# A four-layer convolution network on one core: results held until loads have come, foldings spread later, another order of the set-up, last masks on VectorE

## The chip, the cores and the metric

The kernel runs on one core of a Trainium2 chip. A core has a matrix engine (TensorE, "PE" in the profile; "PEld" is its loading of weights), a vector engine (VectorE, "DVE"), a scalar engine (ScalarE, "ACT"), a general engine (GpSimd, "POOL") and an engine that here only issues transfers (SyncE, "SP"). Each runs its own list of instructions in order and waits at an instruction until what it needs is there. Transfers between DRAM and the core's memory are issued by SP, ACT or POOL and are carried out by 16 DMA engines that they share. PE writes its products to PSUM, a small memory of eight banks; ACT and DVE take them out.

The metric is device time in microseconds (us). Eight runs of the kernel before took 3073.03 to 3084.0 us, with a median of 3080.26 us.

## The reference

The input x has 1024 images of 16 x 16 pixels and 16 channels (float32). Four layers follow one another, each added to its input; ahead of each stands a normalisation by groups of two channels per image.

```python
x = x + L0(gn(x))   # tensor-train matrix on the 16*16*16 values: three cores of rank 16
x = x + L1(gn(x))   # depthwise filters, dense 48->128, relu, dense 128->16, mask
x = x + L2(gn(x))   # 3x3 convolution, 16 -> 16 channels, and a bias
x = x + L3(gn(x))   # as L1, with other weights

def _gn(v, G=8, eps=1e-5):          # mean and variance over height, width and 2 channels
    return (g - m) / jnp.sqrt(s + eps)

def update(x):                      # layers 1 and 3, one step
    p = concat([xt, depthwise(xt, conv1), depthwise(xt, conv2)])   # 48 channels
    d = relu(p @ fc0_w.T + fc0_b) @ fc1_w.T + fc1_b
    xn = xt + d
    return xn * (alive(xt) & alive(d))   # alive: 3x3 maximum of channel 3 above 0.1
```

## The kernel before, in words

**Data.** The images are cut into two chunks of 512. A chunk is 32 "lines" of 128 partitions by 512 images (256 KB each). Two big buffers of 32 lines, X0 and X1 (`XN`), hold a chunk each; between layers the results lie in DRAM (`xf[1]` to `xf[4]`; `xf[3]` is the same memory as `xf[2]`, layer 2 adds to it in place).

**How the order comes about.** The order on every engine is the order in which the program writes the instructions. `run` (from line 1478) takes a layer as a list of steps of PE, and lays background lists (loads, norms, preparation of weights) between them: each background step has a cost or is a pause, and is written out when the layer's steps have come to its share of the window given. Pauses are shrunk so that they fill at most 0.7 of the window. `now` writes a list out at once. All that is fixed is the order on each engine: an engine that is not held up by data runs ahead of the others.

**Set-up** (lines 1529 to 1546). SP loads x of chunk 0 in eight pieces of 1 MB; DVE takes statistics of each (`stat`, L833). `setup[0]` transposes the weights of layer 0; `setup[1:]` are the sums of `c0` on POOL (L535 to L541) and eight steps `gs` that multiply two cores (PE L560, ACT L564) and store the result (SP L569). `lines[0]` and `lines[1]` turn the pixels of the upper and lower half into lines: four transposes on PE (L839) and a copy on ACT (L842, which stays in X0, or L850), and POOL stores them to `xr` (L844, L852). `tail` makes the norm's factors: `small` (DVE aggregate L864, ACT root L866), `newton`, two `widen` (DVE L880), two `spread` (PE L888, ACT L889). Then `start` builds the first weights (PE L1020, ACT L1025, DVE L1038), and `normed` (DVE L910) makes the input of the first product (PE L1097). PSUM's tag `w` has four banks, which the copies of transposes, of `pg`, of `pw` and of the foldings share in turn.

**Layer 0** runs in five phases of 16 units. In phase 1 (160 steps of two products) the weights of layers 1 and 3 are prepared in the background: `beside(make1, make3)` alternates the steps of both layers. The first eight of each are inputs, two dense ones, bias lines and rows, `taps` (DVE L331, POOL L335 and L337), `order` (POOL L350, L359) and `xpats` (POOL L321 to L324). Then eleven foldings follow, each a `make` (PE L392 into two banks, ACT L398 into a buffer `e`) and a `send` (2 to 16 transfers by POOL, L404, 80 per layer). Each layer has three buffers `e`, used in turn, so a folding's copy waits until the sends of the folding three before it have landed. The buffers lie in X1; at 0.75 of the phase SP loads the next part into X1 (L939).

**Layers 1 and 3** (`layer_nca`) work through 32 tiles a chunk, (q, w2) with q from 0 to 3 and w2 from 0 to 7: products L1465, relu on ACT L1468, products L1318, DVE adds bias and input (`u`, L1330), and `residual` multiplies by the mask and adds to the tile fetched from DRAM, both on POOL (L1367, L1368). Some steps later SP stores the tile (L1370); in the last chunk of layer 3 PE transposes it instead (L1377), DVE copies it (L159), and SP stores the output (L1607).

**Layer 2** (`layer_conv`) has 16 rows h a chunk. PE multiplies (L1192 and, across the halves, L1201), ACT adds the bias and writes a result `r` (L1240; twelve buffers), and POOL sends it with an accumulating transfer to `xf[2]` (L1243). The program writes the sends out late, from h = 5 on, but nothing else stands between them on POOL. Beside chunk 0 SP loads chunk 1 into X1 (16 pieces of 512 KB, L784) and DVE and ACT normalise it: sum of all pieces (L598, L606, L614), mean on PE (L693), subtraction (L639), squares, variance (L697). Beside chunk 1 the next layer's chunk 0 is loaded into X0 (L791) and normalised by quarters (L722, L726, L738).

Of the kernel before, what the change touches and what calls it, by code (L numbers as in the profile page):

```python
# [12 lines left out]
ALU = mybir.AluOpType  # L13
# [9 lines left out]
NL = 32  # L23
# [80 lines left out]
def conv_preact_kernel(ctx: ExitStack, tc: tile.TileContext, a: dict, out: bass.AP):  # L104
    nc = tc.nc
    V, A, G, T = nc.vector, nc.scalar, nc.gpsimd, nc.tensor
# [9 lines left out]
    xf = [  # L116
        [dram.tile([8, 4, P, NB], F32, tag=f"xf{l}_{n}", name=f"xf{l}_{n}") for n in range(NCH)]
        for l in range(5)
    ]
# [45 lines left out]
    def cst(name, shape, dt=F32):  # L165
        return const.tile(shape, dt, tag=name, name=name)
# [249 lines left out]


    b2 = cst("b2", [P, 1])

    convw = cst("convw", [P, 512])  # L420

# [360 lines left out]
    def load_wc(X, src):  # L782
        return [
            lambda wh=wh, h=h: nc.sync.dma_start(X[:, 16 * wh + h : 16 * wh + h + 2], rows_wc(src, wh, h, 2))  # L784
            for wh in range(2)
            for h in range(0, S, 2)
        ]

    def load_cw(X, src):
        return [  # L790
            lambda q=q, w=w: nc.sync.dma_start(  # L791
                X[:, 8 * q + w : 8 * q + w + 2], src[w : w + 2, q].rearrange("w p b -> p w b")
            )
            for q in range(4)
            for w in range(0, 8, 2)
        ]
# [5 lines left out]
    def rows_wc(t, wh, h, n=1):  # L802

        t = t[4 * wh : 4 * wh + 4].rearrange("w q (c h) b -> (w q c) h b", h=S)
        return t[:, h : h + n]
# [347 lines left out]
        hw=convw[:, 384:512].rearrange("p (n e m) -> p n e m", n=2, e=2),  # L1153
    )

    def layer_conv(X, n):

        st = {}  # L1160
# [70 lines left out]

            return go

        waiting = []

        def finish(h):

            for wh in range(2):
                r = work([P, NB], "r", "conv")
                A.activation(r, st["po", h][wh], AF.Identity, bias=b2)  # L1240
                waiting.append((rows_wc(xf[2][n], wh, h), r.unsqueeze(1)))
            while waiting and 2 * h + 2 - len(waiting) < 4 * (h - 4):
                G.dma_start(*waiting.pop(0), accum_op=ALU.add)  # L1243

        steps = []
        for h in range(0, S, 2):
# [10 lines left out]
    def layer_nca(X, n, l, L, xo=None):  # L1257


        st = {}  # L1260
# [103 lines left out]

        def residual(q, w2):
            u, r = st["u", q, w2], st["r", q, w2]
            G.tensor_tensor(u, u, st["m"][:, w2], ALU.mult)  # L1367
            G.tensor_tensor(r, r, u, ALU.add)  # L1368
            if xo is None:
                after(7, lambda: nc.sync.dma_start(tile_cw(xf[l + 1][n], 8 * q + w2), r))  # L1370
            else:
                after(8, lambda: turn(q, w2, r))
# [136 lines left out]
    def put(L):  # L1509
        return lambda: nc.sync.dma_start(pack, L["pack"])  # L1510
# [7 lines left out]
    def now(steps):  # L1518
        for step in steps:
            step = step[1] if isinstance(step, tuple) else step  # L1520
            if callable(step):
                step()

    def beside(xs, ys):

        pause = [12, 8, 1, 1, 6, 14, 10, 6] + [1] * (len(xs) - 8)
        return [z for x, y, t in zip(xs, ys, pause) for z in (x, 2.6, y, 2.6, t)]

    L1, make1 = nca_weights("L1_conv_", X1[:, 0:16])
    L3, make3 = nca_weights("L3_conv_", X1[:, 16:32])  # L1530
    with ExitStack() as es:
# [5 lines left out]

        A.activation(work([P, NB], "n", "warm")[:, 0:1], ident[:, 0:1], AF.Sqrt)
        now(setup[:1])
        now(stat[0] + stat[1])  # L1540
        now(setup[1:])
        now(lines[0][:4] + lines[1][:4] + tail[:3] + lines[0][4:10] + tail[3:])
        start, phases = layer_train()
        start()
        now(normed(0, 0, 1) + combined(0, True))
# [42 lines left out]
    with ExitStack() as es:  # L1588
        shared[0] = "m"
        stage(es, conv_sb, conv_ps)  # L1590
        run(layer_conv(X0, 0), 108, load_wc(X1, xf[2][1]), (norm_lines(X1), 0.09, 1.04), by=0.07)
        run(
            layer_conv(X1, 1), 108, load_cw(X0, xf[3][0]) + [put(L3)], (norm_cw(X0, True), 0.09, 1.06), by=0.07
        )
    with ExitStack() as es:
        shared[0] = "o"
# [41 lines left out]
```

## Time and profile before

| what | value |
|---|---|
| median of 8 runs | 3080.26 us (3073.03 to 3084.0) |
| profiled execution, its own time | 3077.39 us |
| its span, first to last instruction | 3075.7 us |
| mean granted clock of TensorE | 0.985 |
| PE busy | 2988.1 us (97%), 13746 instructions |
| PEld busy | 1250.5 us (41%) |
| DVE busy | 1756.8 us (57%) |
| ACT busy | 1099.8 us (36%) |
| POOL busy | 684.8 us (22%) |
| DMA | 418.67 MB, mean 136 GB/s |

How it is read: the stages lie at about 0 to 45 us (set-up), 45 to 1810 (layer 0; phase 1 from some 212 to 559), 1810 to 2296 (layer 1), 2296 to 2526 (layer 2), 2526 to the end (layer 3). A line of the timeline gives the start and length of a group of instructions in us, the engine, the line in the kernel, the operation, what it writes and reads, how many there are, and in brackets how long the engine stood before it and what ended that. A line of waits gives the waiting engine and line, what it waited for, the total, the number and the longest. "Issue" as a releaser means that the profile shows nothing that was waited for. DMA-issuing instructions of SP are not counted as busy.

### The profile page before, as it was taken

How to read it: one execution, taken by the hardware profiler on the slowest of the kernel's cores; microseconds unless marked ns; L12 is line 12 of the kernel's file. 1: busy time of each engine (PE TensorE's matmuls, PEld its weight loads, DVE VectorE, ACT ScalarE, POOL GpSimd, SP SyncE). 2: the span in 40 equal slices, each digit the busy share in tenths (PEclk: the TensorE clock that was granted, in tenths of full speed). 3: DMA queues.
4: the chain of work that ended last, by engine and by line, in shares of the span. 5: the costliest groups of instructions: out<-in, count | busy, mean ns of one | idle time of the engine just before them, and what ended most of it. 6: DMA issues, size and time to landing. Idle time of an engine off the chain costs nothing.

```text
span 3075.7 us, 36641 instructions
## 1 busy us (share of the span) xinstructions
PE 2988.1 (97%) x13746; PEld 1250.5 (41%) x13746; DVE 1756.8 (57%) x2330; ACT 1099.8 (36%) x1798; POOL 684.8 (22%) x738
## 2 busy tenths in 40 slices
PE   7999899999999999999999999999998999999996
PEld 5544334444444444444444433333333333333332
DVE  5264236555554555544555668656967766856432
ACT  4431331100000000000101156666676656666563
POOL 2125651200000000000000015434542223442332
PEclk8999999999999999999999999999999999999998
DMA  7644654533333433322222244435346756344555
GB/s 297 233 129 96 142 115 159 178 108 110 112 112 126 149 108 108 108 101 87 87 87 93 70 142 160 130 129 195 123 136 150 190 92 208 123 129 115 149 162 195
DMA packets 251809, 418.67 MB, mean 136 GB/s; under 512 B 35044, under 2 KB 105320, under 8 KB 248560
## 3 DMA queue, kind: packets, MB, share of 16 engines
q1 hardware_dynamic: 225376, 362.45, 35.8%
q0 software_dynamic: 25440, 53.58, 8.5%
q8 instruction: 109, 1.79, 0.2%
q14 instruction: 68, 0.56, 0.1%
q10 hardware_dynamic: 816, 0.30, 0.0%
HBM read 238.79 MB, written 165.60 MB: 131 GB/s over the span
## 4 chain that ended last, share of the span: by engine, by line
issue 47%; PE 34%; POOL 4%; DMA 1%; DVE 1%; SPq 0%; POOLq 0%; DVEq 0%
PE ph L1465 17%; PE po L1318 6%; PE po L1097 6%; PE po L1192 2%; POOL u L1367 2%; POOL res L1368 2%; POOL xf L1243 1%; PE ptx L1377 0%; PE L_conv_pe L392 0%; PE pw L1020 0%; PE pvar L726 0%; DMA xn<-xf 0%; PE pr L738 0%; PE pmean L722 0%; PE po L1201 0%
## 5 line engine op out<-in xcount | busy, mean ns | idle before, releaser
L1097 PE MATMUL po<-xn,w 128*128 128x512 f32 x3584 | 1579.2, 597 | 4.6 <-DVE xn L910 4.6
L1097 PEld LDWEIGHTS po<-xn,w 128*128 128x128 f32 x3584 | 671.0, 190 | 843.0 <-issue 820.3
L1468 ACT ACTIVATE hid<-ph,pack 128x512 f32<-128x512 f32 x1024 | 652.6, 686 | 381.3 <-PE ph L1465 271.7
L1133 DVE TENSOR_TENSOR r<-r,po 128x512 f32<-128x512 f32 x576 | 377.9, 683 | 593.2 <-PE po L1097 526.4
L1367 POOL TENSOR_TENSOR u<-u,mask 128x512 f32<-128x512 f32 x128 | 203.2, 1587 | 1817.1 <-DMA nx<-xn 1263.4
L1025 ACT COPY w<-pw 128x512 f32<-128x512 f32 (+1 forms) x320 | 150.6, 557 | 1189.3 <-issue 1003.4
L1465 PE MATMUL ph<-xn,wq 32*128 32x512 f32 x3664 | 567.8, 611 | 0.0
L1465 PEld LDWEIGHTS ph<-xn,wq 32*128 32x128 f32 x3664 | 233.2, 184 | 270.6 <-issue 237.6
L1465 PE MATMUL ph<-xn,pack 32*128 32x512 f32 x1288 | 298.8, 626 | 1.2 <-DVE mask L1363 0.9
L1318 PE MATMUL po<-hid,pack 128*32 128x512 f32 x2048 | 281.9, 605 | 2.7 <-ACT hid L1468 2.7
L1038 DVE TENSOR_TENSOR w<-w 128x512 f32<-128x512 f32 x320 | 210.3, 683 | 93.7 <-ACT w L1025 93.7
L639 DVE TENSOR_TENSOR xn<-xn,m 128x1024 f32<-128x1024 f32 x160 | 225.4, 1457 | 45.6 <-ACT m L654 45.5
L1368 POOL TENSOR_TENSOR res<-res,u 128x512 f32<-128x512 f32 x128 | 212.4, 1659 | 10.0
L1330 DVE SCALAR_TENSOR_TENSOR u<-po,pack,xn 128x512 f32<-128x512 f32 x128 | 95.9, 749 | 204.4 <-PE po L1318 200.3
L1192 PE MATMUL po<-xn,convw 128*128 128x512 f32 x368 | 166.6, 605 | 5.1 <-ACT conv L1240 5.1
L1465 PEld LDWEIGHTS ph<-xn,pack 32*128 32x128 f32 x1288 | 116.3, 186 | 98.9 <-issue 63.1
L1133 DVE TENSOR_TENSOR xn<-xn,po 128x512 f32<-128x512 f32 x96 | 64.3, 684 | 125.9 <-PE po L1097 125.8
L1318 PEld LDWEIGHTS po<-hid,pack 128*32 128x32 f32 x2048 | 42.8, 108 | 198.0 <-issue 138.2
L606 DVE TENSOR_TENSOR sq<-sq 128x1024 f32<-128x1024 f32 x78 | 106.9, 1370 | 13.9 <-ACT sq L624 11.7
L1192 PEld LDWEIGHTS po<-xn,convw 128*128 128x128 f32 x368 | 69.1, 193 | 102.7 <-issue 93.6
L1020 PE MATMUL pw<-R,gq 32*128 32x256 f32 (+1 forms) x1280 | 91.4, 385 | 13.2 <-ACT xn L398 10.9
L404 POOL DMA_DIRECT2D L_conv_wy<-xn x160 | 88.9, 563 | 42.4 <-ACT xn L398 31.7
(162 smaller groups left out, 1773.0 us busy)
## 6 DMA issues: line engine op xcount, KB each, us to landing
xf<-r SPq DMA_DIRECT2D x112, 512.0 KB, 3.9
xn<-xf SPq DMA_DIRECT2D x96, 512.0 KB, 5.2
r<-xf SPq DMA_DIRECT2D x80, 512.0 KB, 4.5
wq<-L_conv_wy SPq DMA_DIRECT2D x192, 192.0 KB, 2.8
res<-xf SPq DMA_DIRECT2D x128, 256.0 KB, 3.1
xf<-res SPq DMA_DIRECT2D x96, 256.0 KB, 2.0
res<-xr SPq DMA_DIRECT2D x256, 64.0 KB, 2.8
xf<-conv POOLq DMA_DIRECT2D x64, 256.0 KB, 5.9
```

Of the source, the lines that this page charges most:

```text
L606: V.tensor_tensor(st["t"], st["t"], x, ALU.add)
L639: V.tensor_tensor(part, part, m().unsqueeze(1).broadcast_to([P, 2, NB]), op)
L1025: A.copy(w[:, k0:4, :, 32 * r : 32 * r + 32].rearrange("p k t (v o) -> p v (k t) o", v=2), pw[r],)
L1038: V.tensor_tensor(w[:, k], w[:, x], w[:, y], ALU.add if sign > 0 else ALU.subtract)
L1097: T.matmul(po, st["w", u][:, matrix, t], x, start=t == 0, stop=t == 3)
L1133: V.tensor_tensor(r[at], r[at], po, ALU.add if sign > 0 else ALU.subtract)
L1192: T.matmul(st["po", h][wh], conv["fw"][:, y], X[:, 16 * wh + h + y - 1], start=y == max(0, 1 - h), stop=y == min(2, S - h),)
L1318: T.matmul(po[32 * j : 32 * j + 32], nca["w1"][:, v], hid[j], start=v == 0, stop=v == 1)
L1367: G.tensor_tensor(u, u, st["m"][:, w2], ALU.mult)
L1368: G.tensor_tensor(r, r, u, ALU.add)
L1465: T.matmul(ph, w, x, start=k == 0, stop=k == len(tiles) - 1)
L1468: A.activation(h, ph, AF.Relu, bias=nca["bt"][:, r : r + 1])
```

## The change

There are four parts. In layer 2 the list of waiting sends is gone; each send is written out beside its result, and ahead of a chunk's first one POOL copies one element of the last line of the buffer that is being loaded, so that POOL waits there for that load. In `beside`, the pause inside a folding's pair falls from 2.6 to 1.6, and the last pause ahead of the foldings rises from 6 to 18. In the set-up, the first four turns of the upper half go ahead of the sums and `gs`, `small` goes ahead of the first four turns of the lower half, and six more turns go behind the rest of `tail`. In `residual`, the last tile of each chunk, (3, 7), goes to DVE (`V`) instead of POOL (`G`).

```diff
+    come = cst("come", [1, 1])
...
-    def layer_conv(X, n):
+    def layer_conv(X, n, other):
...
-        waiting = []
-
         def finish(h):
 
+            if h == 0:
+                G.tensor_copy(come, other[0:1, NL - 1, 0:1])
             for wh in range(2):
                 r = work([P, NB], "r", "conv")
                 A.activation(r, st["po", h][wh], AF.Identity, bias=b2)
-                waiting.append((rows_wc(xf[2][n], wh, h), r.unsqueeze(1)))
-            while waiting and 2 * h + 2 - len(waiting) < 4 * (h - 4):
-                G.dma_start(*waiting.pop(0), accum_op=ALU.add)
+                G.dma_start(rows_wc(xf[2][n], wh, h), r.unsqueeze(1), accum_op=ALU.add)
...
         def residual(q, w2):
             u, r = st["u", q, w2], st["r", q, w2]
-            G.tensor_tensor(u, u, st["m"][:, w2], ALU.mult)
-            G.tensor_tensor(r, r, u, ALU.add)
+
+            by = V if (q, w2) == (3, 7) else G
+            by.tensor_tensor(u, u, st["m"][:, w2], ALU.mult)
+            by.tensor_tensor(r, r, u, ALU.add)
...
     def beside(xs, ys):
 
-        pause = [12, 8, 1, 1, 6, 14, 10, 6] + [1] * (len(xs) - 8)
-        return [z for x, y, t in zip(xs, ys, pause) for z in (x, 2.6, y, 2.6, t)]
+        pause = [(2.6, t) for t in (12, 8, 1, 1, 6, 14, 10, 18)] + [(1.6, 1)] * (len(xs) - 8)
+        return [z for x, y, (s, t) in zip(xs, ys, pause) for z in (x, s, y, s, t)]
...
-        now(stat[0] + stat[1])
-        now(setup[1:])
-        now(lines[0][:4] + lines[1][:4] + tail[:3] + lines[0][4:10] + tail[3:])
+        now(stat[0] + stat[1] + lines[0][:4] + setup[1:] + tail[:1] + lines[1][:4] + tail[1:] + lines[0][4:10])
...
-        run(layer_conv(X0, 0), 108, load_wc(X1, xf[2][1]), (norm_lines(X1), 0.09, 1.04), by=0.07)
+        run(layer_conv(X0, 0, X1), 108, load_wc(X1, xf[2][1]), (norm_lines(X1), 0.09, 1.04), by=0.07)
...
-            layer_conv(X1, 1), 108, load_cw(X0, xf[3][0]) + [put(L3)], (norm_cw(X0, True), 0.09, 1.06), by=0.07
+            layer_conv(X1, 1, X0), 108, load_cw(X0, xf[3][0]) + [put(L3)], (norm_cw(X0, True), 0.09, 1.06), by=0.07
```

## The prediction

> **What bounds the kernel now.** TensorE (PE) is busy for 2988.1 of 3075.7 us, so only its idle time, and what its clock loses after it, can be won. I read the waits of PE first, then each large one in the timeline of its engines, then the stretches around it.
>
> The waits of PE (engine, line, releaser; us in total, times, longest):
> ```profile
> PE pw L1020 <- ACT xn L398: 10.9, 1, 10.9
> ...
> PE pmean L693 <- DVE s1s L614: 8.9, 1, 8.9
> ...
> PE po L1097 <- DVE xn L910: 4.6, 1, 4.6
> PE pvar L726 <- DVE s2s L614: 3.2, 1, 3.2
> PE ptx L1377 <- POOL res L1368: 2.9, 1, 2.9
> ```
> Each line is one single stall, and each of the four parts of the change touches one of them: foldings (10.9), layer 2 (8.9 and 3.2), set-up (4.6), last tile (2.9). The first, in the foldings, by the timelines of PE, ACT and POOL:
> ```profile
> 314.84 1.15 PE L1020 MATMUL pw<-R,gq 32*128 32x256 f32 x16
> 338.05 1.58 PE L1020 MATMUL pw<-R,gq 32*128 32x256 f32 x16
> ...
> 359.31 0.70 PE L1020 MATMUL pw<-R,gq 32*128 32x256 f32 x4
> 370.87 2.55 PE L1020 MATMUL pw<-R,gq 32*128 32x256 f32 x12 [10.86 <-ACT xn L398]
> ...
> 397.48 1.57 PE L1020 MATMUL pw<-R,gq 32*128 32x256 f32 x16
> ```
> ```profile
> 356.70 2.15 ACT L398 COPY xn<-L_conv_pe 36x512 f32<-36x512 f32 x4 [14.54 <-DMA L_conv_wy<-xn]
> 369.15 2.15 ACT L398 COPY xn<-L_conv_pe 36x512 f32<-36x512 f32 x4 [10.30 <-DMA L_conv_wy<-xn]
> ```
> ```profile
> 346.38 16.14 POOL L404 DMA_DIRECT2D L_conv_wy<-xn  x29
> 365.12 0.56 POOL L404 DMA_DIRECT2D L_conv_wy<-xn  x1 [2.59 <-issue]
> 365.89 33.78 POOL L404 DMA_DIRECT2D L_conv_wy<-xn  x61 [0.21 <-issue]
> ```
> POOL reaches the first sends only at 346.38; the fourth folding of each layer needs the buffer of the first, whose 32 sends are out by 367.0. ACT stands in its copy until 369.15, the banks stay full, PE stands.
>
> The second, in layer 2: DVE sums the lines as they land, PE waits for the sum.
> ```profile
> 2318.52 1.23 DVE L606 TENSOR_TENSOR s<-s,xn 128x1024 f32<-128x1024 f32 x1 [1.61 <-DMA xn<-xf]
> 2321.11 1.23 DVE L606 TENSOR_TENSOR s<-s,xn 128x1024 f32<-128x1024 f32 x1 [1.37 <-DMA xn<-xf]
> ...
> 2334.54 1.23 DVE L606 TENSOR_TENSOR s<-s,xn 128x1024 f32<-128x1024 f32 x1 [1.39 <-DMA xn<-xf]
> 2335.80 0.69 DVE L614 TENSOR_TENSOR s1s<-s 128x512 f32<-128x512 f32 x1
> ```
> ```profile
> 2301.00:2315.00 14.00, 13.47 (x33) 4.98 (x32) 8.26 (x7) 12.71 (x14) 4.16 (x5) 1.00 0.98 368
> 2315.00:2334.00 19.00, 12.65 (x33) 4.86 (x32) 8.89 (x8) 7.62 (x9) 3.42 (x4) 0.89 1.08 293
> ```
> The last two columns of these stretches are DMA share and GB/s. The engines are full in both, but pieces (512 KB) come every 2.6 us in the second; POOL issued eight accumulating results from 2310.22 on, each as soon as ACT had written it.
>
> **Set-up: +4.0.** The sequence on ACT before:
> ```profile
> 35.74 0.25 ACT L866 ACTIVATE small<-small 128x32 f32<-128x32 f32 x1
> 35.87 3.04 ACT L850 COPY lines<-ptin 128x512 f32<-128x512 f32 x6
> 38.72 1.17 ACT L889 COPY xn<-ptmr 128x512 f32<-128x512 f32 x2
> 40.83 1.20 ACT L1025 COPY w<-pw 128x256 f32<-128x256 f32 x4 [0.94 <-ACT xn L889]
> ```
> The root at 35.74 ends the statistics, which follow the last load (DVE waits for it at 30.37). Before, eight copies precede it and six fill the time in which DVE and PE make the spread tiles. Now four precede it (in the dead time near 20 us), four fill that gap, and the six lie behind the spread copies, ahead of the weights. ACT is unbroken from 35.87 to 39.89, so four more copies at 3.04/6 = 0.51 behind the root give +2.0 at least. In order: root to 36.0, four copies to 38.1, the spread copies as before or 0.5 sooner, six copies (3.04), then the weights: +2.6. Mixing (DVE L1038) and the first norm (L910) wait behind the weights, and PE's first product (45.20) behind them. POOL now issues the first 1 MB store ahead of the sums, at some 22 us, while loads still run at 420 GB/s: the last load is late by 0 to 2.5. POOL's sums and the stores of g (SP) come some 2 to 3 us later, covered, as the weights they feed are wanted 3 later too. Ends 2.0 and 5.5; a gain is excluded by ACT's unbroken row. I take 4.0. Phase 0 behind it has PE at 49.1 to 50.0 of 50 us, so it all stays.
> [...]
>
> **Foldings: -12.7.** Nothing is removed; 60 small steps (eight preparing ones and 22 of foldings for each of two layers) move against PE's steps (two products, 1.72 us). Pauses inside the foldings fall from 2.6 to 1.6, the one ahead of them rises from 6 to 18, and since the planner shrinks all pauses until they fill 0.7 of the window (factor 0.77 before, 0.89 now), the eight steps ahead move later too: taps from step 24 to 27, the first folding from 44 to 54, the fourth from 64/66 to 72/73, the last from 113 to 113. POOL runs freely and is started by DVE's copies in taps (264.87), which now follow step 27's product: +6.2 us. Its chain (taps, order, patterns) is its own issue time and landings, so sends begin at 352.6 and the second first-folding is in at 375.4. PE, with only six foldings ahead, is at the weights of step 70 at 356.9, and needs the late banks after step 79, at 376.5, where it now stands 0.5 us, and again some 2 for the weights of step 80, because ACT runs its fourth and fifth foldings back to back. The stall unit took 397.48-359.31 = 38.17; one with the same four foldings took 338.05-314.84 = 23.21. So 15.0 is there to win (10.9 idle, the rest half clock), less 2.3. Later foldings have their buffers in time: POOL is through by some 455, as PE reaches the loads of part 1 (SP, 470.0 before) with as much slack as before, one step less. For PE's 0.5 and 2 the bound from below is none at all (if POOL's idle 2.59 stays away). Ends: -15.0, and 0 if POOL is so late that the stall moves whole.
>
> **Layer 2: -10.3 and -2.5.** POOL gets one copy of one element per chunk, which waits for the last piece; behind it on POOL stand the 32 sends, behind them only ACT's result buffers (12). Without the sends pieces come at 512 KB over 412 GB/s (5 us window from 2305) = 1.27 us, DVE's add takes 1.275: from 2306.16 less 2.1 (last part) the sum is through at 2324.3, and PE, which comes to the mean at 2327.65, doesn't wait. That is 8.9, and 1.9 of slow clock (L693 2.0 against 0.86, L1201 2.63 against 1.84). I leave 0.5 for slower pieces. The sends start at 2324 with eight results waiting; ACT fills twelve at 2335. The 5.1 us wait of PE on ACT's results at 2373 stays, since ACT is unbroken from 2356 on. In chunk 1, PE's wait for the variance (3.25, with 1.5 of slow clock behind it) loses the 1.5 us that DVE waited for pieces 5 and 7: -2.5, ends 0 and -4.7. For chunk 0 the ends are -10.8 and, if pieces stay at 2.6, -2.
> The copy itself has no row; the nearest are POOL's smallest copies, 0.2 us each (L350): nothing.
> On the clock: a wait of 3.25 us was followed by 0.66, one of 2.17 (2417.7) by 1.00. [...]
>
> **Last tile: -1.3.** Four times two POOL operations (1.2 to 2.1 us each) become two on DVE, at the 0.69 of its other 128x512 operations (L1133; L1363 with the mask's type: 0.69). At the end of the kernel the result (POOL done 3051.13) is there at 3049.9, but DVE's two copies of the tile before come behind it; the last copies end 1.3 sooner, and the 22.3 us of final stores start so. Ahead of layer 2 it starts the loads 2.1 sooner (counted). DVE's last norm operation and flags come 1.4 later, covered: PE is at 50 of 50 us from 2050 on. Ends -2.0 and 0.
>
> **Sum.** +4.0-12.7-10.3-2.5-1.3 = -22.8. The profiled execution took 3077.4, so 3054.6; the median shown is 2.9 above it: 3057.5.
>
> **Rivals.**
> POOL too late again: sends begin 15 us later, not 6.2, as POOL's waits for pattern landings (315 to 346) stretch; the stall keeps its 15 us. For it: 2.59 us of unexplained idle in the sends; against: the chain hangs on nothing moved but the taps. 3070, chance 0.12.
> The hold doesn't speed the loads: if pieces are slow for another reason (the stretch is already full at 368 GB/s before), or the copy is released early, layer 2 gives 2. Against: the pace changes just behind the sends. 3068, 0.11.
> The hold backs up, slower: POOL may not send until the last piece; ACT needs the thirteenth buffer at 2343.9, so the piece must land by 2337 (0.87 to issue, 5.9 to land). Each us later stops ACT and PE for one. From 2366 on (loads half as fast as now) it eats all gains: 3087, 0.07. Now they are in by 2334.5 with the sends among them.
> Two of these halves at once, with the set-up at its upper end: 3074 to 3086, 0.08.
>
> **Numbers.** Forecast 0.62, alone 3050 to 3066. With the first two rivals faster is 0.85; within 0.2% (6 us, about what a measurement tells) 0.08; slower 0.07. The range takes the forecast's bounds and both of those rivals: 3046 to 3073.
>
> **What would show it.** PE's first product at some 49; no wait of PE on ACT L398 above 3 us; pieces every 1.3 us and no wait at L693; POOL's sends of a chunk starting with a row of about eight, just after the last piece; the last transposes no longer waiting 2.9 for POOL. The prediction is wrong if PE's wait on L398 is still near 10, or DVE's adds still wait 1.4 each.

## The result, and the profile after

Eleven runs of the changed kernel have a median of 3057.96 us (3052.06 to 3061.56), 31 runs of the kernel before 3078.95 (3070.48 to 3086.66). The ratio is 0.9926, with a 95% interval of 0.9916 to 0.9937: some 21 us less. The forecast was 3057.5. The profiled execution took 3055.69 us, its span is 3054.0 against 3075.7; TensorE's busy time hardly moved (2986.6 after 2988.1), so some 20 of the 21.7 us gained are idle time, as hoped for. Line numbers of the two kernels differ by one in most places.

The waits of PE after the change (us in total, times, longest):

```profile
PE pc L522 <- DMA core<-in_L_conv_core_dram: 9.6, 1, 9.6
PE po L1193 <- ACT conv L1241: 5.1, 1, 5.1
PE po L1098 <- DVE xn L911: 4.6, 1, 4.6
...
PE ptx L1378 <- DVE res L1369: 1.9, 1, 1.9
...
PE ptmr L889 <- DVE wide L881: 1.5, 1, 1.5
PE pvar L727 <- DVE s2s L615: 1.3, 1, 1.3
```

The largest wait, 9.6 at the kernel's start for the weights of layer 0 (pc), is as it was (9.7 before); no part of the change touches it. Of the stalls that the change was meant for, 10.9 on a folding and 8.9 on pmean are gone, and the last transposes' wait fell from 2.9 on POOL to 1.9 on VectorE. The variance's wait (pvar) fell from 3.2 to 1.3, but a second profile of the kernel before has 1.0 there (below). The 5.1 of layer 2 stayed, as predicted.

Waits do not show the clock, so the two spans were also cut at instructions that both kernels have. "P" is the pw of phase 1's sixth long unit (before: 294.02), "Q" the last pw of phase 1.

| stretch, us | before | after | difference | predicted |
|---|---|---|---|---|
| start to PE's first product | 45.20 | 48.81 | +3.61 | +4.0 |
| first product to P | 248.82 | 248.66 | -0.16 | 0 |
| P to Q (foldings) | 263.75 | 253.32 | -10.43 | -12.7 |
| Q to layer 2's first product | 1738.22 | 1738.41 | +0.19 | 0 |
| layer 2 | 230.11 | 216.56 | -13.55 | -12.8 |
| layer 3 to the issue of the last stores | 527.28 | 525.92 | -1.36 | -1.3 |
| last stores | 22.3 | 22.3 | 0 | 0 |

They add up to -21.7, the difference of the spans. Of layer 2's 13.55, chunk 0 has 10.2 and chunk 1, from its first product on, 3.4. These two profiles are called the first pair below. Only one row is off by more than 1 us, the foldings.

**Foldings.** PE's timeline in phase 1, the unit that came out long and the one behind it:

```profile
336.73 1.15 PE L1021 MATMUL pw<-R,gq 32*128 32x256 f32 x16
338.58 1.54 PE L392 MATMUL L_conv_pe<-xn 9*36 9x512 f32 x8 [0.70 <-ACT w L1026]
340.05 3.06 PE L1098 MATMUL po<-xn,w 128*128 128x512 f32 x4
343.04 1.94 PE L392 MATMUL L_conv_pe<-xn 9*36 9x512 f32 x8
344.91 10.20 PE L1098 MATMUL po<-xn,w 128*128 128x512 f32 x20
...
364.28 1.15 PE L1021 MATMUL pw<-R,gq 32*128 32x256 f32 x16
...
387.49 1.58 PE L1021 MATMUL pw<-R,gq 32*128 32x256 f32 x16
```

The unit from 364.28 to 387.49 takes 23.21, with no wait: the residual stall of 2.3 us that the prediction set aside at steps 79 and 80 did not come. But the unit ahead of it takes 27.55, with only 0.70 of idle time. Four products of po take 3.06 there against 1.98 elsewhere (369.98 in the same phase). PE's windows in that place (width, busy, then granted clock, DMA share, GB/s):

```profile
340.00:342.00 2.00, 2.00 (x6) 0.70 0.73 228
342.00:344.00 2.00, 2.00 (x10) 0.50 0.56 148
344.00:346.00 2.00, 2.00 (x10) 0.50 0.88 340
346.00:348.00 2.00, 2.00 (x4) 0.59 0.17 24
```

PE is busy throughout and runs at half clock for some 7 us. That is a new loss, in which no wait of the page shows. POOL's sends began at 352.84, where the forecast had 352.6. But the forecast's times of phase 1 leave out that the set-up starts the phase later, and P came 3.45 us later than before. Counted from P, the sends began at 55.4, against 52.4 before and 58.6 by the forecast: 3.2 sooner than thought.

**Set-up.** ACT's timeline after:

```profile
35.76 0.23 ACT L867 ACTIVATE small<-small 128x32 f32<-128x32 f32 x1 [2.71 <-DVE small L866]
35.90 2.03 ACT L843 COPY xn<-ptin 128x512 f32<-128x512 f32 x4
38.68 0.59 ACT L890 COPY xn<-ptmr 128x512 f32<-128x512 f32 x1 [0.75 <-PE ptmr L889]
39.53 0.59 ACT L890 COPY xn<-ptmr 128x512 f32<-128x512 f32 x1 [0.27 <-PE ptmr L889]
40.39 3.09 ACT L851 COPY lines<-ptin 128x512 f32<-128x512 f32 x6 [0.27 <-PE ptin L840]
44.43 1.20 ACT L1026 COPY w<-pw 128x256 f32<-128x256 f32 x4 [0.96 <-ACT lines L851]
```

The root is where it was, then come four copies, the spread copies, six copies of lines and the first weights, 3.6 later than before (40.83). The last statistics start at 30.40 (30.37 before): POOL's early store of 1 MB did not delay the last load. The store was issued at 21.82 and landed at 33.25, behind the last load.

**Layer 2.** Chunk 0 by POOL, DVE and PE:

```profile
2316.05 0.18 POOL L1238 COPY come<-xn 1x1 f32<-1x1 f32 x1 [26.47 <-DMA xn<-xf]
2316.56 7.17 POOL L1242 DMA_DIRECT2D xf<-conv  x8 [0.34 <-issue]
```
```profile
2299.49 17.85 DVE L607 TENSOR_TENSOR s<-s,xn 128x1024 f32<-128x1024 f32 x14
2317.37 0.69 DVE L615 TENSOR_TENSOR s1s<-s 128x512 f32<-128x512 f32 x1
```
```profile
2320.70 1.02 PE L694 MATMUL pmean<-s1s,gm_wc 128*128 128x512 f32 x2
```

POOL stands 26.47 us for the last piece, DVE adds fourteen pieces without a gap at 1.275 each (before: the last eight 2.6 or more apart), the sum is there at 2318.1 and pmean starts at 2320.70 with no wait. Behind the copy eight sends go out in a row.

### The profile page after: what moved, and what is told of

Read it like the earlier page. It is cut to its first block, busy times and chain, and to the rows that moved or that the text cites. A ratio compares the mean times of both kernels' runs of the same rounds, so it can differ in the third digit from the quotient of the medians.

```text
span 3054.0 us, 36639 instructions
## 1 busy us (share of the span) xinstructions
PE 2986.6 (98%) x13746; PEld 1251.2 (41%) x13746; DVE 1757.7 (58%) x2338; ACT 1100.4 (36%) x1798; POOL 675.7 (22%) x732
## 4 chain that ended last, share of the span: by engine, by line
PE 82%; issue 8%; POOL 5%; DMA 1%; DVE 1%; ACT 0%; SPq 0%; POOLq 0%; DVEq 0%; ACTq 0%
PE po L1098 51%; PE ph L1466 16%; PE po L1317 6%; PE pw L1021 3%; POOL res L1369 2%; POOL u L1368 2%; PE po L1193 2%; PE L_conv_pe L392 1%; POOL xf L1242 1%; PE ptin L840 1%; PE ptx L1378 1%; DMA xn<-xf 1%; PE pr L739 0%; PE pmean L723 0%; PE pvar L727 0%
## 5 line engine op out<-in xcount | busy, mean ns | idle before, releaser
L1368 POOL TENSOR_TENSOR u<-u,mask 128x512 f32<-128x512 f32 x124 | 196.0, 1580 | 1818.0 <-issue 1230.4
```

The source lines that it names most:

```text
L1368: by.tensor_tensor(u, u, st["m"][:, w2], ALU.mult)
```

## The experiments

Each run has one profile; its stretches, cut as above, are in one table at the end of this section. Executions of one kernel differ by several us (the changed one: 9.5 from lowest to highest), so where a few us matter the verdict is read from the stretch and not from the total. The runs were made in groups, each with its own runs of the kernel before, whose medians go from 3075.52 to 3079.24; medians of different groups thus compare to some 4 us only. All edits are made in the changed kernel, but for two runs of which it is said.

### The set-up: which half costs

The whole order of before:

```diff
-        now(stat[0] + stat[1] + lines[0][:4] + setup[1:] + tail[:1] + lines[1][:4] + tail[1:] + lines[0][4:10])
+        now(stat[0] + stat[1])
+        now(setup[1:])
+        now(lines[0][:4] + lines[1][:4] + tail[:3] + lines[0][4:10] + tail[3:])
```

> The changed kernel with the set-up in the order of the kernel before; the other three edits stay. The new order moved TensorE's first product (the first po <- xn, w of phase 0) from 45.20 to 48.81 us, 3.6 later. Theory (the order alone did that): the first product comes back to 45.2, and the whole run is 3.6 us shorter than the changed kernel's, about 3054.3. Rival (the later start is absorbed later on, because POOL's late store of x to DRAM and its loads then hold up something in phase 0): the first product comes back to 45.2 but less than 1.5 us of it is left at the start of phase 1.

Only the second half undone:

```diff
-        now(stat[0] + stat[1] + lines[0][:4] + setup[1:] + tail[:1] + lines[1][:4] + tail[1:] + lines[0][4:10])
+        now(stat[0] + stat[1] + lines[0][:4] + setup[1:] + lines[1][:4] + tail[:3] + lines[0][4:10] + tail[3:])
```

> The changed kernel with only the second half of the set-up's reordering undone: the first four turns (the first lines of tile row 0) stay ahead of the rest of the set-up, as in the change, but the weights' root goes back behind the lower turns (after tail[:3]) and the late lines back ahead of the tail's end. Theory (what costs is ScalarE: six copies of lines now stand between the spread copies and the mixing, from 40.39 to 43.48 us): the first product returns to about 45.2, 3.6 us sooner, and the whole run to about 3054.3. Rival (what costs is the early turns with POOL's store of 1 MB ahead of the last load's statistics): the first product stays at 47 to 49 and the run within 1.5 us of 3058.

With the whole order undone the first product did not come back to 45.2: it came at 49.05, and the median (3057.84) is that of the changed kernel. PE and ACT of this run:

```profile
18.96 14.02 PE L561 MATMUL pg<-cores,xn 16*128 16x128 f32 x64
32.91 8.67 PE L840 MATMUL ptin<-ident,xn 128*128 128x128 f32 x56
```
```profile
39.56 0.25 ACT L867 ACTIVATE small<-small 128x32 f32<-128x32 f32 x1
39.69 3.04 ACT L851 COPY lines<-ptin 128x512 f32<-128x512 f32 x6
42.54 1.18 ACT L890 COPY xn<-ptmr 128x512 f32<-128x512 f32 x2
```

pg took 14.02 us against 10.93 in the first profile of before. In the old order the root stands on ACT behind eight copies of transposes, which stand on PE behind pg; so when pg is slow, the root is late, 39.56 in place of 35.74. The old order is thus not a fixed 45.2. Its five profiles give 45.20, 46.28 and 45.23 (pg 10.93, 11.53, 10.96) and 49.05 and 48.37 (pg 14.02 twice), 46.8 on average. Six profiles of the new order give 47.91 to 50.60, 49.4 on average: there the root waits for DVE (2.71 us in the first pair) and not for PE, but the six copies of lines cost their time whether pg is slow or not. The changed order costs 2.6 us on average, less than the 3.6 of the first pair.

These 2.6 are the sum of two effects that the profiles show apart. The root comes 1.4 sooner on average (35.65 to 36.26 in the new order, 35.73 to 39.56 in the old). From the root to the first weights, start to start, ACT takes 5.09 to 5.13 us in all five profiles of the old order and 7.76 to 10.00 in the six of the new one, 4.0 more on average. That part goes with PE: the 24 transposes (ptin) behind ptmr, which the six copies wait for, take from 2.78 us (7.76) to 4.86 (10.00), and the two lengths have the same order in all six.

With half of it undone the first product came at 46.18, although the last statistics began at 31.37 in that run, 1 us later than in the others; in the second run with this order at 47.77 with pg at 11.61. From the root to the first weights it is 5.06 and 5.48 us. So the theory's cause holds (the copies behind the spread copies), and the early turns cost nothing that can be seen. The totals don't show it: the ratio to the kernel before is 0.9927, with 0.9926 for the changed kernel. That the store of 1 MB holds up the last load by 1 to 2.5 us is refuted: in the nine profiles with it the last statistics began at 30.69 on average (30.28 to 31.37), in the five without at 30.34 (29.94 to 30.64). The averages differ by 0.35, less than either group's own range.

### The foldings

The pauses of before:

```diff
-        pause = [(2.6, t) for t in (12, 8, 1, 1, 6, 14, 10, 18)] + [(1.6, 1)] * (len(xs) - 8)
-        return [z for x, y, (s, t) in zip(xs, ys, pause) for z in (x, s, y, s, t)]
+        pause = [12, 8, 1, 1, 6, 14, 10, 6] + [1] * (len(xs) - 8)
+        return [z for x, y, t in zip(xs, ys, pause) for z in (x, 2.6, y, 2.6, t)]
```

> The changed kernel with the foldings' pauses of the kernel before; the other three edits stay. Phase 1's stretch from the pw of its third unit to the start of phase 2 was 10.4 us shorter in the changed kernel. Theory (the pauses removed a stall of 15.0 us in which a folding waited for its spread copies, and brought in one place of half clock, 4.3 us): the stall comes back, TensorE again waits over 10 us on one folding, and the run is 10.4 us longer, about 3068.4. Rival (part of those 10.4 us comes from the set-up's new order, which moves POOL's work ahead of phase 1): the stall is shorter than 12 us and the run under 3065.

The last long pause raised:

```diff
-        pause = [(2.6, t) for t in (12, 8, 1, 1, 6, 14, 10, 18)] + [(1.6, 1)] * (len(xs) - 8)
+        pause = [(2.6, t) for t in (12, 8, 1, 1, 6, 14, 10, 22)] + [(1.6, 1)] * (len(xs) - 8)
```

> The changed kernel with the last long pause of the foldings raised from 18 to 22. No folding then stands right behind a pw product in TensorE's order; in the changed kernel one did at 336.73 to 340.1 us (pw with 32 rows, 1.15 us, then the folding with 9 rows, 1.54 us), and the granted clock read 0.50 from about 342 to 346. The unit that holds it took 27.55 us where one without took 23.21. Theory (the two low-row groups in a row pull the clock down): no stretch of 0.5 in phase 1, that unit 23.2 to 24, the run 3.6 to 4.3 us shorter than the changed kernel's, about 3054. Rival (the drop has another cause, such as the number of foldings in one unit or the 0.70 us wait for ScalarE's w): a drop of the same kind stays in phase 1 and the run is within 1.5 us of 3058. Third case: the spread copies come too late for the foldings, which now start a unit sooner, and TensorE waits at the first of them.

With the old pauses the stall came back, but shorter, and the run's median was 3063.38, +5.4. PE, and the start of POOL's sends:

```profile
369.25 2.55 PE L1021 MATMUL pw<-R,gq 32*128 32x256 f32 x12 [7.11 <-ACT xn L398]
```
```profile
344.68 16.18 POOL L404 DMA_DIRECT2D L_conv_wy<-xn  x29
```

P to Q is 260.16 against 263.75 before. That looked like the rival (the set-up's order reaches into phase 1), but the kernel before with the last tile's edit alone, whose set-up is the old one, gives 259.91 with a wait of 6.91; a second profile of the kernel before gives 263.76 with 11.16. Two of four lie at 264 and two at 260, one of each set-up at 260. What goes with it is the start of the sends: 8.33 and 8.30 us behind the pw ahead of them in the long two, 4.51 and 4.64 in the short two. So the stall's length hangs on POOL's chain, as the prediction had it, and one wait in that chain (L323, 4.25 and 4.20 in the long two, 1.99 and 1.98 in the short two) makes part of the difference. From DVE's copies in taps (L331) to the first send the chain took 81.5 us in the long two and 77.7 and 77.8 in the short two. Why it has two lengths stays open. In the ten profiles with new pauses it took 77.3 to 78.9, so how those would do with a chain of 81.5 is not shown.

With 22 the unit at 338.14 took 23.99 and P to Q 249.15. This one run could not tell the fix from luck: the changed kernel's own foldings, in five more profiles, gave 250.02, 250.02, 250.03 and 250.02, and once 253.36. The unit with the folding right behind pw took 27.55, 25.90 and four times 24.26. Against 23.21, 1.05 is always lost there (0.70 of it the wait for the weights), and the rest, 3.29 and 1.64, is the clock, by chance. With 22, P to Q came out at 249.15 and three times at 248.35 or 248.36. So the pause of 18 costs a fixed 1.7 us (1.05 here, 0.6 at a second such place), and the clock took 3.3 more in two of its six runs. With 22, one of four lost 0.8 in a pw that took 1.93 in place of 1.15; no cause shows for it. The fixed part comes from the order and the wait and not from the clock: in the run with the set-up of before the unit took 24.26 with the clock at 1.00 from 333 to 353. The theory, that two groups with few rows in a row lower the clock, fits the rest, but two of six runs against none of four do not prove it.

### Layer 2's hold

No hold:

```diff
-            if h == 0:
-                G.tensor_copy(come, other[0:1, NL - 1, 0:1])
```

> The changed kernel without the copy that POOL makes before layer 2's first send: each pair of results goes out as soon as ScalarE has it (the kernel before held the first four pairs back by its list). In the changed kernel POOL stood 26.47 us at that copy in chunk 0 and 28.81 in chunk 1, and the two chunks together came out 13.6 us shorter than before. Theory (the sends that add into DRAM slow the loads of the other chunk, DVE falls behind with its sums and TensorE waits at pmean): the pieces come at 2 to 2.7 us in place of 1.3, TensorE waits 6 to 9 us at pmean in chunk 0 and 1 to 5 in chunk 1, the clock drops behind the wait, and layer 2 is 10 to 16 us longer than the changed kernel's, the whole about 3068 to 3074. Rival (the gain came from the pieces' order and not from the hold, as sends and loads have room enough side by side): layer 2 within 2 us of the changed kernel's.

Half of it:

```diff
-                G.tensor_copy(come, other[0:1, NL - 1, 0:1])
+                G.tensor_copy(come, other[0:1, NL // 2 - 1, 0:1])
```

> The changed kernel with the copy on POOL waiting for the eighth of the other chunk's sixteen pieces in place of the last. Held to the end, pieces came every 1.27 us and pmean did not wait; not held at all, they came every 2.6 and pmean waited 4.40. Theory (the sends that add into DRAM share the DMA engines with the loads, whenever they run): the first eight pieces come every 1.27 us, then the results saved up go out in a row and the rest come every 2.6, some 10 us more, of which about 2.6 are slack: pmean waits 6 to 9 us, layer 2 comes out 8 to 11 us longer than the changed kernel's and longer than with no hold. Rival (a shorter hold is enough, since only the first sends among the first loads hurt): pmean waits under 3 us and layer 2 is within 3 us of the changed kernel's 216.

Without the hold DVE and PE read:

```profile
2308.26 1.22 DVE L607 TENSOR_TENSOR s<-s,xn 128x1024 f32<-128x1024 f32 x1 [1.36 <-DMA xn<-xf]
2310.88 1.23 DVE L607 TENSOR_TENSOR s<-s,xn 128x1024 f32<-128x1024 f32 x1 [1.39 <-DMA xn<-xf]
```
```profile
2321.46 2.07 PE L694 MATMUL pmean<-s1s,gm_wc 128*128 128x512 f32 x2 [4.40 <-DVE s1s L615]
```

Pieces come every 2.6 us once sends are under way, pmean waits 4.40 and its products run at half speed (2.07 against 1.02). Layer 2 takes 222.96, 6.4 more than the changed kernel's, and the ratio to the kernel before is 0.9963 after 0.9926. The cause is the theory's for chunk 0, which takes 113.47 in place of 106.24. The size is under its 10 to 16, since the loads now also start sooner than before (the last tile, below). For chunk 1 the theory missed: the variance was to wait 1 to 5 us and waits 0.52, and the chunk takes 109.48, no more than with the hold (110.3).

With half the hold POOL was let go at 2303.39, eight sends followed by 2314, and the last four pieces came every 2.6 us:

```profile
2318.66 1.23 DVE L607 TENSOR_TENSOR s<-s,xn 128x1024 f32<-128x1024 f32 x1 [1.38 <-DMA xn<-xf]
```
```profile
2320.67 1.12 PE L694 MATMUL pmean<-s1s,gm_wc 128*128 128x512 f32 x2 [2.25 <-DVE s1s L615]
```

A wait of 2.25 and 220.31 for layer 2, +3.75, all of it in chunk 0. The theory missed, and of the rival's two signs the wait under 3 came and layer 2 within 3 us did not: fewer pieces were slowed than the theory counted, as most had landed by 2308, but the last four, which met the sends, came 2.6 us apart in place of 1.275. Of the three lengths tried in the changed kernel, holding to the last piece is the only one with no wait at pmean.

### The last tile

POOL again, in the changed kernel:

```diff
-            by = V if (q, w2) == (3, 7) else G
+            by = G
```

> The changed kernel with the last tile's two masking operations of every chunk back on POOL. Theory (only the very last tile of the program is on the path that sets the end): the last transposes (ptx) again wait about 2.9 us for POOL's result in place of 1.9 for VectorE's, the time from the first product of layer 3 to the issue of the final stores grows by 1.4 us, and the whole by 1.4, to about 3059.4 against a median of 3058. Rival (the same tile at the end of each chunk of layers 1 and 3 also holds up the next chunk's load or product): each chunk's end costs the same, four times in all, and the whole grows by 4 to 6 us.

And the edit alone, made in the kernel before:

```diff
+            by = V if (q, w2) == (3, 7) else G
-            G.tensor_tensor(u, u, st["m"][:, w2], ALU.mult)
-            G.tensor_tensor(r, r, u, ALU.add)
+            by.tensor_tensor(u, u, st["m"][:, w2], ALU.mult)
+            by.tensor_tensor(r, r, u, ALU.add)
```

> The kernel before with one of the four edits, the last tile of a chunk masked by VectorE. Set-up, foldings and layer 2's list are the old ones, so each of their stages gives a third sample of the old state. Theory: the first product at 45 to 49 us, by chance of the clock; phase 1 from the pw of its sixth long unit to its last pw again 263.7 us with a wait of about 11 us on one folding (263.75 and 263.76 in two profiles of the kernel before; 260.16 with the old pauses in the changed kernel); pmean in chunk 0 waits less than 8.9 us, as layer 1's last tile goes out 2.1 us sooner and the other chunk's loads with it; layer 3 to the issue of the final stores 526.0 in place of 527.4; the whole 2 to 4 us less than the kernel before. Rival for the stall (it is decided by chance and not by the set-up's order): anything from 260 to 264. Rival for pmean (the loads' start does not matter, the sends among them do): 8.9 again within 0.5.

With POOL the end reads as before:

```profile
3035.53 1.12 PE L1378 MATMUL ptx<-ident,res 128*128 128x128 f32 x4 [2.90 <-POOL res L1369]
```

Layer 3 takes 527.54, with VectorE 526.0 in nearly all profiles: 1.5, as expected. Layer 2 is 216.14 with a pmean wait of 0.22, so beside the hold the later start of the loads costs almost nothing. The median of five runs, 3061.73, is 3.8 above the changed kernel's, between the theory's 1.4 and the rival's 4 to 6. But these runs go from 3054.95 to 3062.10, and by the stretches only layer 3 grew by what the edit explains. (The profiled run, 3061.74, lost 5 us or more to the clock in phase 0: from 110 to 120 us it read 0.50 with PE busy throughout.)

Alone, the edit does more than 1.3:

```profile
2333.65 2.08 PE L693 MATMUL pmean<-s1s,gm_wc 128*128 128x512 f32 x2 [5.14 <-DVE s1s L614]
```

pmean waits 5.14 in place of 8.90 and 9.23, since layer 1's last tile is stored sooner and the other chunk's loads start on that: 3.1 us behind layer 2's first product in place of 5.2. Chunk 0 takes 112.94 (before 116.41 and 117.18). Ten runs have a median of 3072.39, a ratio of 0.9983 (0.9974 to 0.9992). That is 5 us less than the runs of the kernel before beside it (3077.45); 2 to 4 were expected. The two edits thus do part of the same work in chunk 0: with neither it takes 116.41 and 117.18, with the mask alone 112.94, with the hold alone 106.41, with both 106.24.

### The kernel before once more, and the mends

The kernel before, unchanged:

> The kernel before once more, for a second profile: how much of the set-up's and the stall's length is chance. In its first profile the first product came at 45.20 us and TensorE waited 10.86 us on one folding. With its set-up order in the changed kernel the first product came at 49.05, as pg ran at half speed from its start and the copies of x stand ahead of the root on ScalarE; with its pauses in the changed kernel the wait was 7.11. Theory (both lie in the spread of executions): the first product anywhere from 45 to 49.5, the wait anywhere from 7 to 11. Rival (both are of the kernels, not of the execution): 45.2 and 10.9 again within 0.5.

The stall came again at the same length, P to Q 263.76; the first product at 46.28. So neither was quite right: the stall has two lengths and this was the long one again, the set-up varies (pg took 11.53 us after 10.93).

The second profile also bears on what chunk 1 of layer 2 is worth. The variance in the kernel before, unchanged, and in the run without the hold:

```profile
2446.21 1.05 PE L726 MATMUL pvar<-s2s,gv_cw 128*32 128x512 f32 x2 [1.02 <-DVE s2s L614]
```
```profile
2430.01 1.04 PE L727 MATMUL pvar<-s2s,gv_cw 128*32 128x512 f32 x2 [0.52 <-DVE s2s L615]
```

The first profile of the kernel before waited 3.25 there. Chunk 1 takes 113.70 and 109.99 in the two profiles of the kernel before, 112.74 in the one with the last tile's edit alone (a wait of 2.11), and 109.48 without the hold. In eight of the nine profiles with the whole hold it takes 109.3 to 110.7, in one 112.78, with a wait of 2.12. So this wait is long or short from one execution to the next, with the hold and without. The averages, 111.5 of the four without it and 110.3 of the nine with it, leave some 1 us for the hold, which is not shown. The rest of the 3.4 us that chunk 1 gave in the first pair is chance.

Both mends (the second half of the set-up undone, pause 22), then 22 with the whole old order:

> The changed kernel with two mends at once: the weights' root back behind the lower turns of the set-up (as in the run with half of the set-up undone), and the foldings' last long pause at 22 (no folding right behind a pw). Theory (the two are independent): the first product at 45 to 46.5 us, phase 1 from the pw of its sixth long unit to its last pw in 249 to 250 us (253.3 in the changed kernel's profile, 250.0 and 253.4 in two other runs of the same foldings), together 4 to 6 us less than the changed kernel, a median of about 3053. Rival (the clock drops somewhere else instead, since what decides it is chance): the first product is earlier but the median is within 2 us of 3058.

> As the run with both mends (median 3048.9), but with the whole set-up in the order of the kernel before, not only its second half. Theory (the first half of the new order, with the first four turns ahead of pg, takes the copies of x off ScalarE's path to the root, so it is worth something when pg runs at half speed from its start): the first product between 45 and 49.5 us as the clock falls, 47 on average and no sooner than with the half; the median 0 to 2 us above that of the run with both mends, about 3050. Rival (the early turns cost, since POOL's store of 1 MB runs among the last loads): the median 1 to 3 us below it, about 3047.

The first has a median of 3048.87 (six runs, 3046.55 to 3051.44; ratio to the kernel before 0.9906, 0.9890 to 0.9922), the second 3051.26 (five runs, 3048.30 to 3055.91; 0.9923, 0.9909 to 0.9936). Both have P to Q at 248.4. The first product came at 47.77 and 45.23. The first of these was expected at 45 to 46.5, with a median of about 3053, the second no sooner than the first; these missed. The totals don't separate the orders.

Last, 22 and the six late turns behind the start of the first unit:

```diff
-        now(stat[0] + stat[1] + lines[0][:4] + setup[1:] + tail[:1] + lines[1][:4] + tail[1:] + lines[0][4:10])
+        now(stat[0] + stat[1] + lines[0][:4] + setup[1:] + tail[:1] + lines[1][:4] + tail[1:])
         start, phases = layer_train()
         start()
-        now(normed(0, 0, 1) + combined(0, True))
+        now(lines[0][4:10] + normed(0, 0, 1) + combined(0, True))
```

> The changed kernel with the foldings' last long pause at 22, and with the six late turns of the set-up (lines[0][4:10]: their transposes on TensorE and their copies on ScalarE) moved behind the start of the first unit, so that the root, the spread copies and the first weights follow each other on ScalarE; the root stays ahead of the lower turns, as in the change. Theory (the six copies of lines, 40.39 to 43.48 us, are the only reason why the changed kernel's first product is late): pw starts right after ptmr at 39 to 39.5 in place of 42.57, the first product comes 6.24 us behind it, at 45.2 to 46, whether pg runs at half speed or not, and the median is 3047 to 3050. Rival (the work moved is only paid later: the six turns come between the first weights and the first products, and the second weights wait for them): the first product is at 45 to 46 but the start of phase 1's sixth long unit, 248.2 to 250.2 us behind it in all other runs but one, comes 2 us later against it, and the median stays at 3049 to 3052.

```profile
42.07 5.38 PE L840 MATMUL ptin<-ident,xn 128*128 128x128 f32 x24
47.24 2.03 PE L1098 MATMUL po<-xn,w 128*128 128x512 f32 x4
```

pw began at 40.01 and not at 39 to 39.5, and the first product came at 47.24, since the six turns, moved off ACT's path, now stand on PE's, their 24 transposes taking 5.38 us where the quickest of the new order took 2.78. The third unit's pw follows at 60.55 against 63.88 in the changed kernel, so 3.3 us were won all the same, and the clock took them back once more between 98 and 116: that unit took 17.76 for 14.46, sixteen products of pg in it 3.78 for 2.38, and from 100 to 150 the granted clock was 0.90, in the changed kernel 0.97. The median is 3048.22 (four runs, 3046.07 to 3053.66; 0.9897, 0.9881 to 0.9914), in the range expected, though the first product is not. It and the version with both mends are clearly faster than the kernel before. Against the changed kernel (0.9916 to 0.9937) the interval of this one lies just below, and that of both mends (0.9890 to 0.9922) overlaps a little; what they surely share is the shorter P to Q. Which of the two is better the runs don't tell.

| run (us) | first product | to P | P to Q | Q to layer 2 | layer 2 | of it chunk 0 | layer 3 | profiled | median |
|---|---|---|---|---|---|---|---|---|---|
| before | 45.20 | 248.82 | 263.75 | 1738.22 | 230.11 | 116.41 | 527.28 | 3077.4 | 3078.95 |
| before once more | 46.28 | 250.47 | 263.76 | 1736.87 | 227.17 | 117.18 | 527.48 | 3076.02 | |
| changed | 48.81 | 248.66 | 253.32 | 1738.41 | 216.56 | 106.24 | 525.92 | 3055.69 | 3057.96 |
| set-up of before | 49.05 | 250.14 | 250.02 | 1737.05 | 217.01 | 106.36 | 526.04 | 3053.36 | 3057.84 |
| half of the set-up | 46.18 | 248.28 | 253.36 | 1738.48 | 215.91 | 105.95 | 525.94 | 3052.14 | 3053.79 |
| pauses of before | 47.91 | 248.23 | 260.16 | 1738.37 | 215.51 | 105.71 | 526.04 | 3060.24 | 3063.38 |
| pause 22 | 50.60 | 248.27 | 249.15 | 1738.50 | 215.81 | 105.95 | 526.00 | 3052.34 | 3053.72 |
| no hold | 50.48 | 247.88 | 250.02 | 1737.01 | 222.96 | 113.47 | 526.21 | 3058.57 | 3066.37 |
| last tile on POOL | 49.30 | 255.56 | 250.03 | 1739.15 | 216.14 | 106.41 | 527.54 | 3061.74 | 3061.73 |
| both mends | 47.77 | 248.70 | 248.35 | 1739.20 | 215.46 | 106.16 | 527.95 | 3051.44 | 3048.87 |
| last tile alone | 48.37 | 250.29 | 259.91 | 1738.27 | 225.69 | 112.94 | 526.03 | 3072.58 | 3072.39 |
| half the hold | 49.45 | 250.22 | 250.02 | 1737.07 | 220.31 | 110.19 | 525.86 | 3056.97 | 3062.15 |
| old order, 22 | 45.23 | 248.77 | 248.36 | 1739.29 | 216.58 | 106.17 | 526.02 | 3048.30 | 3051.26 |
| lines last, 22 | 47.24 | 250.28 | 248.36 | 1736.80 | 219.01 | 106.22 | 527.97 | 3053.66 | 3048.22 |

(The two 527.9 in layer 3 come with a granted clock of 0.93 between 2550 and 2600, where the run with the old order has 0.97.)

## Why the prediction was right, point by point

**Set-up, +4.0: right in sign, the parts mis-sized.** The first pair gave +3.61, the averages of all profiles +2.6, both inside the ends of 2.0 and 5.5. But the copies' part (2.6) measured 2.7 to 4.9, 4.0 on average, since the transposes that the copies of lines wait for came late: in the first pair PE ran from 33 to 41 us at a granted clock of 0.50 to 0.57 (1.00 before). The root's gain of 1.4 on average stood in no term. That the average of both comes to 2.6 again is chance. The added term for the last load (0 to 2.5, of which 1.4 was taken) measured 0.03 in the first pair and 0.35 on average. That the old order hangs on how long pg takes (10.93 to 14.02 us), and the new one does not, was not seen either: one profile cannot tell a fixed place from one that chance decides. That the loss stays behind the set-up came true (-0.16 to P), though the row given for it is misread: between 50 and 100 us PE is busy for 46.7 of 50, not 49.1.

**Foldings, -12.7: right mechanism, two terms mis-sized in opposite directions.** The stall went. The steps moved as forecast: DVE's copies in taps came 6.26 us later against P, for 6.2. The chain behind them on POOL, which the prediction took as unchanged, was 3.3 shorter (78.2 us after 81.5), one of the two lengths that it has by chance. So the sends began 3.2 sooner in the phase than forecast; that they agree to 0.3 in the time from the start is luck, as the phase began 3.45 later. The term "less 2.3" for a residual stall at steps 79 and 80 measured 0. Not in the sum was the folding that the new pauses put right behind pw, 1.05 always and up to 4.3 with the clock. Where the clock stayed up (1.00 from 333 to 353 in the run with the set-up of before), the stretch was 13.7 shorter than in the first profile of before, in the first pair 10.4. Nor was the 15.0 to be won a constant: the old stall has two lengths, some 3.7 apart.

**Layer 2, -10.3 and -2.5: chunk 0 right, chunk 1 by luck.** Chunk 0 gave -10.2. The pace without sends (1.27 us a piece), the end of the sum well ahead of PE, eight results waiting and the unchanged 5.1 on ACT are all as forecast. What was wrong is who earns it: 3.8 of the 8.9 come with the last tile's edit too, even without the hold. The prediction had "less 2.1 (last part)" in its working and then booked all of it on the hold. Chunk 1 gave -3.4, but the step that was to bring it, pieces that come faster through the hold, is not shown: the variance's wait is 3.25 and 1.02 in two profiles of the kernel before, 0.52 with no hold and 0.33 to 2.12 with it. Behind the 1.34 that was left in the first pair the clock stayed at 1.00 and the next four products took 1.98. But behind a wait of 2.11 at the same place, with the last tile's edit alone, they took 3.65.

**Last tile, -1.3: right** at the end, -1.4 to -1.5 (the pair and the run with POOL). Its effect on layer 2 is above.

**The sum.** The spans gave -21.7 for -22.8, and the median came within 0.5 us of the forecast. That is nearer than the rows deserve: the foldings were 2.3 short in the first pair, chunk 1's 3.4 were in the main chance, and single runs of the changed kernel lie up to 9.5 us apart.

**Rivals.** POOL too late again: did not happen, no wait on L398's copies is left. That the hold doesn't speed the loads: refuted for chunk 0, 1.275 a piece with it and 2.6 without. That the hold backs up: the last piece came at 2316. By the prediction it would have started to cost at 2337, which is some 2330 here, as layer 2 starts 6.8 us sooner.

## What to carry to other kernels

Where accumulating stores share the DMA engines with loads that someone waits for, try to hold them back until the last load is in: here that was worth 10 us in the chunk where PE waited for the sum, half a hold gave back 4 of them and no hold 7, and in the other chunk no gain is shown. Whether plain stores would slow the loads as much was not tried. When a background list is re-spaced, look also at what the new place stands next to: a folding right behind the weights' products cost 1 us in every run and up to 4 in some. And before a difference of 3 us between two profiles is believed, profile the same kernel twice: here the set-up, a stall and the wait for the variance each had two or more values by chance.

## What the runs showed of the hardware that was not expected

The granted clock fell to half while PE was busy without a gap, or behind 0.26 to 0.70 us of idle time: behind pw (32 rows) and a folding (9 rows) in phase 1 (0.50 from 342 to 346 us in the changed kernel, behind 0.70; 0.57 from 409 to 413 with half of the set-up undone, behind 0.26), and around pg (16 rows) in the set-up (0.50 from 24 to 32 in the kernel before, without a gap) and in phase 0 (0.50 from 106 to 108 in the changed kernel, behind 0.44). In the set-up of the kernel before, the 64 products of pg follow each other without a gap, the first 30 about every 0.11 us, the rest every 0.21. In one and the same unit of phase 0, from its pw at about 100 to the next, profiles read 12.82, 14.46 and 17.76 us. The losses come in steps: 1.64, 3.29, 1.70 in phase 1, 1.64 and 4.94 in phase 0, so about 3.3 us at half speed, or a multiple, by an estimate from these losses. What sets that length was not shown. Whether it is the few rows of these products that lower the clock, no run here tests. In the run with the set-up of before the clock record reads 1.00 throughout pg, although the 64 products took 14.02 us there, one every 0.21 us. The run with the pauses of before has the same pace from 25 to 33 us, 41 products recorded as here, and its record reads 0.50 there. So the pace of the products is the better witness.
